# Gated cross-attention and a mixture of experts on one core: the first expert tile's copy, product and tanh set ahead of the fifteenth token tile's centring, and two experts' weights loaded in steps 10 to 12

## The chip, the core and the metric

The kernel runs on one core of one Trainium2 chip. The core has five engines that run their own instruction streams and meet at semaphores: TensorE (PE in the profile, with its weight loads as PEld), VectorE (DVE), ScalarE (ACT), GpSimd (POOL) and SyncE (SP). Transfers between the chip's memory and the core are issued from the streams of SP, ACT and POOL (SPq, ACTq and POOLq in the profile) and carried by 16 DMA engines. The metric is the device time of one execution in microseconds; lower is better.

## The reference, cut to what matters

There are 8 sequences of 256 tokens with 512 features: 2048 tokens. Each token attends to the memory rows that its sequence's mask leaves open, the result is added with a gate, and then each token passes through 2 of 8 experts.

```python
x = x + jnp.tanh(g_xattn[0]) * _L0_xattn_ref(_layernorm(x, axis=-1), ctx_2048, mask_BxS2_bk0)
x = x + jnp.tanh(g_ffn[0]) * _L0_ffn_ref(_layernorm(x, axis=-1), L0_ffn_w_router, L0_ffn_w_gate, L0_ffn_w_up, L0_ffn_w_down)

# _L0_ffn_ref, on xt of T = 2048 rows:
probs = jax.nn.softmax(xt @ w_router.T, axis=-1)
top_v, top_i = jax.lax.top_k(probs, TOP_K)                  # TOP_K = 2 of 8 experts
top_v = top_v / jnp.sum(top_v, axis=-1, keepdims=True)
comb = jnp.zeros((T, NUM_EXPERTS), dtype=xt.dtype)
comb = comb.at[jnp.arange(T)[:, None], top_i].add(top_v)
g = jnp.einsum('th,eih->tei', xt, w_gate)                   # 512 -> 192
u = jnp.einsum('th,eih->tei', xt, w_up)
act = jax.nn.silu(g) * u
out = jnp.einsum('tei,ehi,te->th', act, w_down, comb)       # 192 -> 512
```

## The kernel before

The work has two stages that overlap. In the token stage a loop over `s` from 0 to 17 takes the 16 tiles of 128 tokens through a software pipeline: tile `s + 1` gets its attention scores (`a_scores`), tile `s - 1` its probabilities (`a_probs`) and its values and sum (`a_values`), and tile `s - 2` is centred (`f_centre`) and squared for the variance (`f_square`). Once per two tiles `f_scale` and `f_weigh` complete the normalised rows, and `f_weigh` stores them with their routing weights into a table in the chip's memory, `xc_d`, by a DMA on ACT's queue (line 444). `f_mark`, `f_rank` and `f_table` build the lists that say which tokens belong to which expert.

In the expert stage each of 36 tiles holds up to 128 tokens of one expert. `gather` (line 639, POOL's queue) fetches a tile's rows from `xc_d` by an index list; `turn` transposes them on PE into `pt_g` (line 192) and copies the result to `xT_g` on ACT (line 194); `gate_up` multiplies with the gate and up weights on PE (line 659, `pgu`), takes a tanh on ACT (line 664) and two products on DVE (lines 665 and 667); `flip` transposes on PE (line 674, `pht`) and copies on DVE; `down` multiplies with the down weights (line 683, `py`), scales on ACT (line 688), and adds the rows into the output by an indirect DMA on POOL's queue (line 689). One call of `step(n)` issues `gate_up` of tile n, `flip` of tile n - 1, `turn` of tile n + 2 and `down` of tile n - 2.

The order of work on every engine is written out by hand: the code of `manual_schedule` is issued in program order, each engine takes its own instructions in that order, and an instruction that waits holds up all that stand behind it on its engine. Three places matter here.

- In step 16 (`s == NT`), `f_centre` and `f_square` of token tile 14 stand near the top, and `turn(order[0])`, the transposes and the copy of the first expert tile, after `a_values(15)`. In step 17, `gate_up(order[0])` and `turn(order[1])` come first, then `f_centre(15)` and `f_square(15)`. So on ACT the first tile's copy stands behind tile 14's centring and squaring.
- The tile lists for the first 8 expert tiles are made early, from the first 10 token tiles (`EARLY = 10`), whose rows are complete in `xc_d` after `f_weigh(4)` in step 13. The gathers of those tiles read only these rows and wait for that store. `fetch` in steps 13 to 16 issues them. The other tiles wait for `f_weigh(7)`, after the last token tile.
- The weights of an expert are loaded in two halves, `load_half(2e)` for gate and up (768 KB) and `load_half(2e + 1)` for down (384 KB). `LOADS` says in which step of the loop each of the first eight halves, those of experts 0 to 3, is issued on SP's queue: steps 3 to 8, and both halves of expert 3 in step 16. The other eight are issued on ACT's queue, one in each of the expert steps 0 to 7. On SP's queue the stores of the attention's result (`x_store`, line 623, two tiles each, in even steps) and the loads of the next sequence's `xT` (line 124) stand in the same program order; an `x_store` waits for DVE's sum of its second tile (line 414).

Of the kernel before, what the change touches and what calls it, by code (L numbers as in the profile page):

```python
# [22 lines left out]
E, I = 8, 192  # L23
T = B * S
TT = S // P
NT = T // P
# [22 lines left out]
def gated_xattn_moe(ctx: ExitStack, tc: tile.TileContext, x, xT, ctxn, ctxT, mask, maskT, g_x, g_f, wr, wgu, wd, out):  # L49
    nc = tc.nc  # L50
# [22 lines left out]
    def row(shape, name):  # L73
        return make(wk, 512, "row", 10, shape, name)
# [64 lines left out]

    def load_half(n):  # L140
        e, part = divmod(n, 2)
        by = nc.sync if n < E else nc.scalar
        if part == 0:
            by.dma_start(out=wgu_sb[:, e * GU:(e + 1) * GU], in_=wgu[:, e * GU:(e + 1) * GU])
        else:
            by.dma_start(out=wd_sb[:, e * DN:(e + 1) * DN], in_=wd[:, e * DN:(e + 1) * DN])
# [269 lines left out]
    def f_centre(i):  # L416
        xr = KEEP["xr", i // 2][:, i % 2, :]
        nc.scalar.activation(xr[:, 0:D], xs[i], AF.Identity, bias=xr[:, NM:NM + 1])  # L418

    def f_square(i):  # L420
        xr = KEEP["xr", i // 2][:, i % 2, :]
        if i % 2 == 0:
            KEEP["ve", i // 2] = sm_.tile([P, 2], FP, tag="ve", bufs=3, name=f"ve_{i}")
        square = row([P, D], f"sq_{i}")
        nc.scalar.activation(square, xr[:, 0:D], AF.Square, scale=2.0 / math.sqrt(D),
                             accum_out=KEEP["ve", i // 2][:, i % 2:i % 2 + 1])
# [198 lines left out]
    def on(f, i, n=NT):  # L625
        if 0 <= i < n:
            f(i)
# [15 lines left out]
    def turn(q):  # L643
        KEEP["xgT", q] = turned(KEEP["xg", q], f"g{q}")
# [4 lines left out]
    def gate_up(q):  # L649
        if q < NS:  # L650
            v = KEEP["own", q] = q if q < E else (q - E) // (LS - 1)
        else:
            v = nc.values_load(eqi[0:1, q - NS:q - NS + 1], engines=[PE], min_val=0, max_val=E - 1,
                               skip_runtime_bounds_check_because="a count of comparisons, at most E - 1")
        KEEP["v", q] = v
        xgT = KEEP.pop(("xgT", q))
        pgu = bank([P, 2 * I], f"pgu_{q}")
        for c in range(HC):
            nc.tensor.matmul(pgu, lhsT=xgT[:, c, :], rhs=span(wgu_sb, v * GU + c * 2 * I, 2 * I),  # L659
                             start=(c == 0), stop=(c == HC - 1))  # L660

        xg = KEEP["xg", q]
        th = half([P, I], f"th_{q}")
        nc.scalar.activation(th, pgu[:, 0:I], AF.Tanh, scale=xg[:, RS:RS + 1])  # L664
        nc.vector.scalar_tensor_tensor(th, th, 1.0, pgu[:, 0:I], ALU.add, ALU.mult)  # L665
        h = half([P, I], f"h_{q}")
        nc.vector.scalar_tensor_tensor(h, th, xg[:, R2:R2 + 1], pgu[:, I:2 * I], ALU.mult, ALU.mult)  # L667
        KEEP["h", q] = h
# [27 lines left out]
    order = [*range(E - 1)]  # L696
# [8 lines left out]
        if 0 <= s < len(order):  # L705
            f(order[s])

    LOADS = (3, 4, 5, 6, 7, 8, NT, NT)
    KEEP["next"], KEEP["known"] = 0, E - 2

    def fetch(upto):
# [3 lines left out]

    def step(s):
        fetch(s + AHEAD)
        if s < E:
            load_half(E + s)
        if s:  # L720
            at(gate_up, s)
        at(flip, s - 1)
        at(turn, s + 2)
        at(down, s - 2)
# [11 lines left out]
    with tc.manual_schedule(engines={PE, DVE, ACT, POOL, SP}):  # L736
        tc.mark_branch_hint_location("long", engines=[PE])
        m_find()
        m_hot(0)
        m_pick(0)  # L740
        m_rows(0, 1)
        m_fetch(0)
        m_count()
        nc.scalar.activation(tg, gates, AF.Tanh)
        constants()
        for p in range(1, NP):
            m_hot(p)
        a_stats(0)
        a_stats(1)
        a_scale(0)  # L750
        r_centre()
        m_hide(0)
        for p in range(1, NP):
            m_pick(p)
        m_rows(1, NP)
        idle = bank([P, D], "idle")
        for n in range(1):
            nc.tensor.matmul(idle, lhsT=ones, rhs=busy, start=True, stop=True)
        v = nc.values_load(many[0:1, 0:1], engines=[PE, DVE, ACT, POOL, SP], min_val=0, max_val=M,
                           skip_runtime_bounds_check_because="rows of a memory")  # L760
        with tc.If(v > CV, label="long") as cmp:
            apart.append({})
            long_way()
        apart.clear()
        with cmp.Else():
            nc.scalar.copy(xs[TT][:, 0:1], cns[0][:, 0:1])
            load_x(TT, 2 * TT)
            load_batch(2)
            load_x(2 * TT, NT // 2)
            load_x(NT // 2, NT)  # L770
        m_mean(0)
        m_centre(0)
        m_turn(0)
        m_gates()
        for s in range(NT + 2):
            odd = s % 2
            p, part = divmod(s, 4)
            on(a_probs, s - 1)
            if s == EARLY + 3:
                f_weigh(EARLY // 2 - 1)  # L780
            if s == EARLY + 2:
                f_close()
            if s == NT + 1:
                gate_up(order[0])
                turn(order[1])
            on(f_centre, s - 2)
            if s:
                if s == 1:
                    a_stats(4)
                on(a_stats, s + 4)  # L790
                if odd:
                    on(a_scale, (s + 3) // 2, NT // 2)
            on(a_scores, s + 1 if s else 0, NT)
            if s == 0:
                for n in range(1, NP):
                    m_fetch(n)
                m_hide(1)
                a_scores(1)
                a_stats(2)
                a_stats(3)  # L800
                a_scale(1)
                more_constants()
                m_route(0)
            if s in (1, 3, 5):
                m_hide(s + 1)
                m_hide(s + 2)
            if part == 1 and p + 1 < NP:
                m_centre(p + 1)
            on(f_square, s - 2)
            if odd:  # L810
                on(f_rank, (s - 3) // 2, NT // 2 - 1)
            if s == EARLY + 3:
                read_table(pick[:, 0:E], 0, E)
            if part == 2 and p + 1 < NP:
                m_turn(p + 1)
            on(a_values, s - 1)
            if s == NT:
                turn(order[0])
            if s == 1:
                nc.tensor.matmul(table, lhsT=ones[0:1, :], rhs=zero[:, 0:P], start=True, stop=True)  # L820
            if odd:
                on(f_weigh, (s - 5) // 2 if s != EARLY + 3 else -1, NT // 2 - 3)
            else:
                on(f_scale, (s - 4) // 2, NT // 2 - 1)
                on(f_mark, (s - 2) // 2, NT // 2 - 1)
                on(f_table, (s - 4) // 2, NT // 2 - 2)
            if s == NT - 4:
                last_constants()
            if s == NT - 2:
                place_rows()  # L830
            if s == EARLY + 1:
                f_total(EARLY // 2 - 1)
            if s == EARLY + 2:
                take_table("early")
            if s == 3:
                no_tokens()
            if s == NT + 1:
                step(0)
                f_weigh(NT // 2 - 3)
                f_weigh(NT // 2 - 2)  # L840
                f_table(NT // 2 - 2)
                f_rank(NT // 2 - 1)
                step(1)
                f_weigh(NT // 2 - 1)
                f_table(NT // 2 - 1)
                take_table("all")
                step(2)
                read_table(pick[:, E:NS], E, NS)
                KEEP["known"] = len(order) - 1
                step(3)  # L850
                f_total(NT // 2 - 1)
                step(4)
                numbers()
                step(5)
                read_table(sel, NS, NQ)
            if part == 0 and p + 1 < NP:
                m_mean(p + 1)
            if part == 0 and 0 < p < NP:
                m_route(p)
            if not odd:  # L860
                on(x_store, (s - 2) // 2, NT // 2)
            if not odd and 3 <= (s + 4) // 2 < B:
                load_batch((s + 4) // 2)
            for n in range(E):
                if LOADS[n] == s:
                    load_half(n)
            if NT - 3 <= s <= NT:
                fetch(2 * (s - NT + 3) + 1)
        for n in range(6, len(order) + 2):
            step(n)  # L870
        more_tiles()
# [31 lines left out]
```

## Time and profile before

| | us |
|---|---|
| three runs | 273.59, 275.84, 276.36 |
| median | 275.84 |
| the profiled execution, whole | 272.73 |
| its span from first to last instruction | 270.8 |
| PE busy | 241.9 (89%) |
| POOL busy | 151.0 (56%) |
| DVE busy | 111.3 (41%) |
| ACT busy | 109.3 (40%) |
| the first expert product (line 659) begins at | 79.76 |
| the last scatter (line 689) is issued at | 262.87 |
| data moved | 48.20 MB, 178 GB/s on average |

The profile is one execution. Its views are a page of sums; a timeline of each engine's instructions; a chain of waits, followed back from the last instruction to whatever released each step; tables of busy time in chosen windows, with the granted TensorE clock (1.00 is full speed) and the busy share of the DMA engines; and the instructions of one source line, with the time from a DMA's issue to its landing. A busy PE is not the same as a PE at its peak. Times inside the profile are counted from the span's start, and the profiled execution is 3.1 us below the median of the three timed ones.

### The profile page before, as it was taken

To read this page: it belongs to the slowest core of one execution; us is meant where nothing else is said; L and a number is where in the kernel's file an instruction comes from. 1 tells how busy PE (TensorE), PEld (TensorE's weight loads), DVE (VectorE), ACT (ScalarE), POOL (GpSimd) and SP (SyncE) were. 2 spreads that over 40 slices of the span, in tenths; PEclk is the share of its full clock that TensorE was granted. 3 is DMA by queue.
4 is the path that set the end of the run, shared out by engine and by line. 5 is a ranking of instruction groups with operands and counts; after the bars stand their busy time and mean duration, and the time that the engine had idled before them with its cause. 6 is when DMAs were issued, how large, how long until landed. Compare 5 with 4: busy or idle time off the path is not lost.

```text
span 270.8 us, 3452 instructions
## 1 busy us (share of the span) xinstructions
PE 241.9 (89%) x998; PEld 149.0 (55%) x998; DVE 111.3 (41%) x451; ACT 109.3 (40%) x264; POOL 151.0 (56%) x243
## 2 busy tenths in 40 slices
PE   4787788879759999999999999999999999999960
PEld 4585565657426655556556555565555555655520
DVE  3448888986974336412213213123122131131310
ACT  2224677777735533333323323333333233333230
POOL 4748899878684055334548384563745745333460
PEclk9999999999997999999999999999999999999995
DMA  4599779995389999884449395595674858326274
GB/s 118 198 340 365 252 236 342 333 336 232 101 273 317 385 312 304 221 178 95 83 82 159 92 168 95 106 173 101 111 155 82 138 112 143 61 39 81 40 94 68
DMA packets 18684, 48.20 MB, mean 178 GB/s; under 512 B 2528, under 2 KB 2528, under 8 KB 18656
## 3 DMA queue, kind: packets, MB, share of 16 engines
q0 software_dynamic: 8416, 21.11, 40.8%
q1 hardware_dynamic: 7040, 17.32, 18.6%
q10 hardware_dynamic: 3200, 9.44, 9.9%
q8 instruction: 12, 0.20, 0.3%
q14 instruction: 16, 0.13, 0.2%
HBM read 29.51 MB, written 18.35 MB: 177 GB/s over the span
## 4 chain that ended last, share of the span: by engine, by line
PE 68%; POOL 10%; DVE 7%; DMA 6%; issue 4%; ACT 3%; SPq 0%; POOLq 0%; ACTq 0%; DVEq 0%
PE pgu L659 34%; PE py L683 21%; PE pt_g L192 6%; POOL ac L491 5%; DMA xh<-x 4%; PE pht L674 3%; POOL out L689 2%; DMA cn<-ctxn,gid 2%; DVE xh L414 1%; PE psc L378 1%; POOL hide L301 1%; DVE st L362 1%; POOL rs L370 1%; PE pc L294 1%; DVE ac L491 1%
## 5 line engine op out<-in xcount | busy, mean ns | idle before, releaser
L659 PE MATMUL pgu<-wgu_sb,xT_g 128*128 128x384 f32 (+1 forms) x288 | 100.9, 494 | 2.9 <-ACT xT_g L194 2.9
L689 POOL DMA_INDIRECT out<-y,ids x36 | 57.1, 1585 | 80.4 <-ACT y L688 25.2
L659 PEld LDWEIGHTS pgu<-wgu_sb,xT_g 128*128 128x128 f32 x288 | 54.7, 192 | 46.7 <-issue 15.3
L683 PE MATMUL py<-wd_sb,hT 96*128 96x512 f32 (+1 forms) x144 | 67.6, 593 | 0.0
L665 DVE SCALAR_TENSOR_TENSOR th<-th,pgu 128x192 f32<-128x192 f32 x36 | 12.8, 354 | 122.7 <-ACT th L664 122.7
L664 ACT ACTIVATE th<-pgu,xh 128x192 f32<-128x192 f32 x36 | 15.1, 420 | 68.9 <-PE pgu L659 63.4
L639 POOL DMA_INDIRECT xh<-xc_d,gids x36 | 35.7, 993 | 12.4 <-issue 7.2
L688 ACT ACTIVATE y<-py,w 128x512 f32<-128x512 f32 x36 | 24.7, 687 | 39.9 <-PE py L683 39.0
L683 PEld LDWEIGHTS py<-wd_sb,hT 96*128 96x128 f32 x144 | 24.5, 190 | 17.8 <-issue 17.5
L194 ACT COPY xT_g<-pt_g 128x512 f32<-128x512 f32 x36 | 21.0, 584 | 8.9 <-PE pt_g L192 8.8
L378 PE MATMUL psc<-cT,xT 128*128 128x137 f32 x128 | 19.6, 302 | 2.5 <-POOL hide L301 1.1
L192 PE MATMUL pt_g<-ident,xh 128*128 128x128 f32 x144 | 21.6, 274 | 0.0
L378 PEld LDWEIGHTS psc<-cT,xT 128*128 128x128 f32 x128 | 17.9, 209 | 5.0 <-issue 2.2
L491 POOL TENSOR_SCALAR ac<-cols,low,idt 128x128 f16<-128x128 f32 x22 | 18.7, 862 | 1.7 <-DVE low L481 1.4
L192 PEld LDWEIGHTS pt_g<-ident,xh 128*128 128x128 f32 x144 | 17.1, 142 | 1.2 <-issue 1.0
L408 PE MATMUL pav<-cn,prT 128*128 128x512 f32 x32 | 16.4, 594 | 0.0
L674 PEld LDWEIGHTS pht<-ident,h 128*96 128x96 f32 x72 | 9.0, 126 | 12.3 <-issue 7.0
L667 DVE SCALAR_TENSOR_TENSOR h<-th,xh,pgu 128x192 f32<-128x192 f32 x36 | 14.9, 415 | 1.3
L509 POOL MEMSET spacer<- 1x1 f32 x25 | 15.2, 610 | 0.0
L676 DVE COPY hT<-pht 96x256 f32<-96x256 f32 x36 | 14.9, 413 | 0.4 <-PE pht L674 0.4
L418 ACT ACTIVATE xr<-xh,xr 128x512 f32<-128x512 f32 x16 | 11.6, 722 | 6.1 <-DVE xh L414 5.5
L674 PE MATMUL pht<-ident,h 128*96 128x128 f32 x72 | 13.8, 273 | 0.0
(187 smaller groups left out, 244.0 us busy)
## 6 DMA issues: line engine op xcount, KB each, us to landing
xc_d<-xr ACTq DMA_DIRECT2D x8, 576.0 KB, 5.2
xT<-xT SPq DMA_DIRECT2D x8, 512.0 KB, 5.9
out<-xh SPq DMA_DIRECT2D x8, 512.0 KB, 4.0
wgu_sb<-wgu SPq DMA_DIRECT2D x4, 768.0 KB, 7.5
wgu_sb<-wgu ACTq DMA_DIRECT2D x4, 768.0 KB, 6.0
xh<-x SPq DMA_DIRECT2D x1, 2048.0 KB, 14.2
wd_sb<-wd SPq DMA_DIRECT2D x4, 384.0 KB, 7.0
wd_sb<-wd ACTq DMA_DIRECT2D x4, 384.0 KB, 5.2
```

The costliest lines, as they stand in the source:

```text
L192: nc.tensor.transpose(pt[:, c, :], src[:, c * P:(c + 1) * P], ident)
L194: nc.scalar.copy(dst, pt)
L378: nc.tensor.matmul(both, lhsT=xTs[b][:, c, t * P:(t + 1) * P], rhs=cTs[p % 2][:, c, :], start=(c == 0), stop=(c == HC - 1))
L408: nc.tensor.matmul(pav, lhsT=prT, rhs=cns[p], start=True, stop=True)
L491: by.tensor_scalar(at_col[:, n, :], cols_w if by is nc.vector else cols, low[:, n:n + 1], idt[:, i, n % 2:n % 2 + 1], ALU.is_equal, ALU.mult)
L509: nc.gpsimd.memset(spacer, 0.0)
L639: nc.gpsimd.indirect_dma_start(out=g, out_offset=None, in_=src, in_offset=bass.IndirectOffsetOnAxis(ap=gids[:, q:q + 1], axis=0))
L659: nc.tensor.matmul(pgu, lhsT=xgT[:, c, :], rhs=span(wgu_sb, v * GU + c * 2 * I, 2 * I), start=(c == 0), stop=(c == HC - 1))
L674: nc.tensor.transpose(pht[:, k, :], h[:, k * IH:(k + 1) * IH], ident)
L683: nc.tensor.matmul(py, lhsT=hT[:, k, :], rhs=span(wd_sb, v * DN + k * D, D), start=(k == 0), stop=(k == 1))
L688: nc.scalar.activation(y, py, AF.Copy, scale=w)
L689: inst = nc.gpsimd.indirect_dma_start(out=out[:, :], out_offset=bass.IndirectOffsetOnAxis(ap=ids[:, q:q + 1], axis=0), in_=y, in_offset=No ...
```

## The change

Four edits, in two groups.

The order of ACT, PE and DVE in steps 16 and 17: `turn(order[0])` in step 16 is now followed at once by `gate_up(order[0])` and `turn(order[1])`, and only then by `f_centre(14)` and `f_square(14)`, which leave their old places in that step. Step 17 keeps `f_centre(15)` and `f_square(15)`. On ACT the order goes from centre 14, square 14, copy 0, tanh 0, copy 1, centre 15, square 15 to copy 0, tanh 0, copy 1, centre 14, square 14, centre 15, square 15. The orders of PE, DVE and POOL stay as they were.

The loads: ten halves instead of eight are issued on SP's queue in the loop. Those of expert 3 move from step 16 to steps 10 and 11, behind `x_store(4)` and the last `xT` load; those of expert 4 move from ACT's queue in expert steps 0 and 1 to SP's queue in step 12, between `x_store(5)` and `x_store(6)`. The remaining six halves stay on ACT's queue, in expert steps 0 to 5 instead of 2 to 7.

```diff
     def load_half(n):
         e, part = divmod(n, 2)
-        by = nc.sync if n < E else nc.scalar
+        by = nc.sync if n < len(LOADS) else nc.scalar
...
-    LOADS = (3, 4, 5, 6, 7, 8, NT, NT)
+    LOADS = (3, 4, 5, 6, 7, 8, 10, 11, 12, 12)
...
     def step(s):
         fetch(s + AHEAD)
-        if s < E:
-            load_half(E + s)
+        if len(LOADS) + s < 2 * E:
+            load_half(len(LOADS) + s)
...
-            if s == NT + 1:
-                gate_up(order[0])
-                turn(order[1])
-            on(f_centre, s - 2)
+            if s != NT:
+                on(f_centre, s - 2)
...
-            on(f_square, s - 2)
+            if s != NT:
+                on(f_square, s - 2)
...
             if s == NT:
                 turn(order[0])
+                gate_up(order[0])
+                turn(order[1])
+                f_centre(s - 2)
+                f_square(s - 2)
...
-            for n in range(E):
-                if LOADS[n] == s:
+            for n, when in enumerate(LOADS):
+                if when == s:
                     load_half(n)
```

## The prediction

> **What bounds the kernel now.** I read the page first, then the chain of waits around the first expert tile, then ACT's timeline there, then windows with clock and DMA share, and last the landing times of single DMAs. The page says that PE carries the end:
>
> ```profile
> PE 241.9 (89%) x998; PEld 149.0 (55%) x998; DVE 111.3 (41%) x451; ACT 109.3 (40%) x264; POOL 151.0 (56%) x243
> PE 68%; POOL 10%; DVE 7%; DMA 6%; issue 4%; ACT 3%; SPq 0%; POOLq 0%; ACTq 0%; DVEq 0%
> ```
>
> From 92 us on PE has no gap until 260 us, one tile every 4.96 us. Whatever brings PE to that stretch earlier or later moves the end by as much: the last scatters follow the last products, so the tail moves along. What matters is how PE gets into the stretch. The chain of waits from 77 to 92 us (start, length, what):
>
> ```profile
> 77.76 0.73 ACT xr L418
> ...
> 79.24 0.48 ACT xT_g L194
> 79.72 0.04 issue
> 79.76 4.43 PE pgu L659 x8
> ...
> 85.65 2.68 PE pgu L659 x8
> ...
> 91.86 0.42 PE pht L674 x2
> ```
>
> The first product waits for the copy of line 194, and the copy stands behind the centring of token tile 14 on ACT. The first product also takes 4.43 us where the second takes 2.68. ACT's timeline shows why the copy is late:
>
> ```profile
> 74.77 0.27 ACT L397 COPY prT<-ppt 128x128 f32<-128x128 f32 x1 [0.50 <-PE ppt L395]
> 77.76 0.72 ACT L418 ACTIVATE xr<-xh,xr 128x512 f32<-128x512 f32 x1 [2.73 <-DVE xh L414]
> 78.52 0.63 ACT L425 ACTIVATE sq<-xr 128x512 f32<-128x512 f32 x1
> ...
> 79.14 0.56 ACT L194 COPY xT_g<-pt_g 128x512 f32<-128x512 f32 x1
> 84.23 0.42 ACT L664 ACTIVATE th<-pgu,xh 128x192 f32<-128x192 f32 x1 [4.53 <-PE pgu L659]
> ```
>
> ACT idles 2.73 us for DVE's sum of tile 14, though the transposes for the copy are done at 76.87 in PE's timeline. The slow product is a matter of the clock (windows; the columns are PE, PEld, DVE, ACT, POOL busy, granted clock, DMA share, GB/s):
>
> ```profile
> 77.46:80.87 3.41, 1.11 (x4) 0.71 (x5) 2.33 (x11) 1.91 (x4) 2.76 (x4) 1.00 0.76 219
> 80.87:84.28 3.41, 3.41 (x8) 1.76 (x7) 0.00 (x0) 0.05 (x1) 2.01 (x4) 0.50 0.94 292
> ```
>
> After a window of 3.41 us in which PE was busy 1.11, the clock is halved for the next 3.41.
>
> **Part 1, the order on ACT.** Nothing is added; the same instructions run in another order. If the rows come as before, the copy starts at 76.9 instead of 79.14, takes 0.56, and the product starts near 77.5: -2.25 us. The two passes that stood ahead (centre and square of tile 14, 77.76 to 79.14, 1.38 us) now stand behind tanh 0 and copy 1. Queued behind them are centre and square of tile 15, copy 2, the three `f_weigh`, and tanh 1. Before, square 15 ends at 86.74, which lets DVE make the last lists until 88.50 and PE take them at 88.82, a slack of 0.3; tanh 1 at 90.55 lets PE flip at 91.86 with no slack (the weight load there waits 0.63 us for DVE's `h`). All of these come 1.38 later after the end of product 0: +1.38 us, with no cover. Centring 14 itself is needed by no one earlier.
>
> **Part 2, the loads in steps 10 to 12.** SP issues 768 and 384 KB behind the `xT` load at 58.65, so at about 59.1 to 60, and as much again behind the store of 64.87, at about 65.3 to 66.5. Together 2.36 MB. At the 396 GB/s of the full window 51 to 53.5 us that is 6.0 us of all DMA engines. They have this much room before:
>
> ```profile
> 62.00:64.00 2.00, 1.76 (x10) 0.92 (x9) 1.79 (x11) 1.45 (x5) 2.00 (x4) 1.00 0.69 269
> 64.00:66.00 2.00, 1.58 (x15) 1.53 (x14) 1.01 (x5) 1.20 (x4) 1.84 (x6) 1.00 0.25 95
> 66.00:68.00 2.00, 1.98 (x15) 1.50 (x15) 1.07 (x8) 1.80 (x8) 1.07 (x8) 1.00 0.57 222
> ```
>
> Idle share times 2 us: 0.62 + 1.50 + 0.86, with 0.1 before and 0.4 after, 3.5 us. So 2.5 us of load work is still outstanding when ACT issues the store of `f_weigh(4)` at 67.86. On this store hangs the first gather, which is now critical: the store lands 2.9 us after issue, at 70.76; the gather starts at 71.66, and its rows land 4.1 later, at 75.76; PE's first weight load for the transposes is at 75.84. Before, these rows waited 2.3 us for ACT; that cover is what Part 1 removes. How does a store fare that is issued behind loads? The same store two steps earlier tells (line 444, issued at 47.0 behind loads of 44.1 to 45.8, and at 67.9 behind none):
>
> ```profile
> L444 ACTq DMA_DIRECT2D xc_d<-xr x1: 379/379/379, 47.0 to 47.0; - x1
> ...
> DMA to landing us min/median/max: 7.8/7.8/7.8
> ```
>
> ```profile
> L444 ACTq DMA_DIRECT2D xc_d<-xr x1: 369/369/369, 67.9 to 67.9; - x1
> ...
> DMA to landing us min/median/max: 2.9/2.9/2.9
> ```
>
> And in the DMA view of 46 to 50 us only SP's queue moves packets:
>
> ```profile
> q1 hardware_dynamic: 308, 1.12, 101.0%
> ```
>
> ACT's store (q10) got nothing until SP's loads were through. **A rule speaks otherwise:** the Trainium skill, "DMA: Bandwidth & Descriptors", section "Queues, rings and completion order", says that each DMA engine goes round-robin between the queues that have work. Then the store, 0.59 MB or 1.5 us, would share half and half and come 1.5 us late. By the trace, first issued first moved, it comes 2.5 late. I take 2.5, the trace's case; the bounds are 0 and 3.0 (none of the last idle usable). With 2.5: gather at 74.16, rows at 78.26, first load 78.34, transposes done about 79.1 (0.60 for four, and 0.14 for the first load), copy 0.56, product at 79.7. Against 79.76: -0.05 us. By the rule it would be 78.7, -1.05. So Parts 1 and 2 together leave PE waiting for rows where it waited for ACT. POOL is also held: `f_scale(5)` and the later gathers start 2.5 later; the third (75.79) then lands at about 82.2, and PE asks for it at about 82.4 at the earliest.
>
> What the loads relieve: SP's loads at 80.55 and 81.06 and two on ACT go from the stretch where the DMA share is 1.0. PE waits for no DMA there before, so this gives nothing by itself. ACT's issue of a `wd` half at 89.60 took 0.84 us, the other three on ACT 0.33 to 0.35, and it stands ahead of tanh 1; with fewer transfers it may shrink: between 0 and -0.5, I take -0.25. Expert 3's and 4's weights are needed from 94.6 and 99.7 us; earlier arrival gains nothing.
>
> **The clock.** Until 76.43 PE is busy, then come 0.6 us of transposes and nothing until 79.7: in 77.46 to 80.87 there would be 0.6 of transposes and 1.2 of product. The windows before show 1.00 kept after 1.99 busy in 3.41 and 0.50 after 1.11; 1.8 lies between. The skill's "TensorE: Matmul & The Clock Gate", Part 4 ("PE-mode transpose"), says that transposes do not count as busy in the same way: then 1.2, and the clock drops as before. I take no change, 0; bounds -1.75 (4.43 against 2.68) and +1.7 (a second window).
>
> **Sum:** -0.05 + 1.38 - 0.25 + 0 = +1.1 us. The profiled execution would go from 272.73 (span 270.8 and 1.9 around it) to 273.8. It lies 3.1 under the median of the runs, 275.84; moved by the same, the median becomes 276.9.
>
> **The rivals.**
> - *Faster: the rows are not late.* The store overtakes or shares, and the product starts between 77.5 and 78.7. Then the window is filled with 2.2 us or more of product, the clock holds, and the sum is -2.25 + 1.38 - 0.25 - 1.75 = -2.9 (273.0), or by sharing -1.05 + 1.38 - 0.25 - 1.75 = -1.7 (274.2). For it: the rule above. Against: the 7.8 us landing. 0.27.
> - *Slower: the first gather also meets the store of tiles 12 and 13.* That store is issued at 72.67 and held the second gather (73.11) to 5.4 us where others take 3.9 to 4.1. The first gather at 74.16 may take its place: +1.3, and with the larger backlog +0.5. Product at 81.5, PE without products for 5 us, which can hold a whole window and so a second one at half clock, +1.7: 1.1 + 1.8 + 1.7 = +4.6, 280.4. It decides once the rows land after 79. Against it: by 74.16 plus the gather's own start most of that store is through. 0.20.
> - *The forecast, but with the clock held:* +1.1 - 1.75, 275.2. It is part of the forecast's 0.53.
>
> That the change doesn't do what it says is excluded: in the instruction lists of both kernels only ACT's four passes and the loads have moved.
>
> **How the numbers follow.** About 1% is what a measurement of this kernel can tell from no change: 273.1 and 278.6. Faster by more: half of the first rival and a little spread, 0.2. Slower by more: the second rival and the upper end of the forecast, 0.3. Within: 0.5. The range runs from the first rival's better end, 273.0, to most of the second, 279.8.
>
> **What would show it.** Right: the first gather starts near 74 and not at 71.7; the store of line 444 issued near 67.9 lands 5 us after issue or later; PE waits ahead of the first transposes, not after them; product 0 begins at 79 to 80; tanh 1 begins 7.5 us or more after product 0 ends, not 6.35. Wrong: product 0 begins before 78.5, or takes 2.7 us, or the store lands in 3 to 4 us. If the step from product 0 to the flip of tile 1 does not grow by 1.1 or more, the cost of the reordered passes is wrong.

## The result: slower, and PE waits for rows that stand behind the loads

| | before | after |
|---|---|---|
| median of 15 executions, us | 275.43 | 278.30 |
| lowest to highest, us | 271.87 to 277.54 | 276.88 to 281.05 |
| ratio of the times | | 1.0151, 95% interval 1.0112 to 1.0189 |
| the profiled execution, whole, us | 272.73 | 277.40 |
| its span, us | 270.8 | 275.6 |

The ratio leaves out executions over 1.5% above the fastest of their kernel, four of before's fifteen and one of after's, so it says +4.1 us where the medians of all fifteen stand 2.9 apart.

The page of the changed kernel (engine, busy us, share, count; then the chain's shares by engine; then two groups with busy us, mean ns and the idle time ahead of them):

```profile
PE 243.1 (88%) x998; PEld 149.5 (54%) x998; DVE 111.2 (40%) x451; ACT 109.3 (40%) x264; POOL 150.7 (55%) x243
...
PE 63%; POOL 10%; DMA 7%; issue 6%; ACT 5%; DVE 4%; ACTq 1%; SPq 1%; POOLq 0%; DVEq 0%
...
L659 PE MATMUL pgu<-wgu_sb,xT_g 128*128 128x384 f32 (+1 forms) x288 | 100.9, 494 | 0.7 <-ACT xT_g L194 0.7
...
L192 PE MATMUL pt_g<-ident,xh 128*128 128x128 f32 x144 | 21.5, 273 | 3.3 <-DMA xh<-xc_d,gids 3.3
```

PE does the same work in almost the same busy time. The new thing is in the last line: all 3.3 us that PE idles ahead of the expert transposes end with a gather's landing. The chain of waits of the changed kernel (start, length, what) shows where that sits, and what follows it:

```profile
68.74 1.40 DMA xc_d<-xr
...
76.96 3.54 DMA xh<-xc_d,gids
80.50 0.14 issue
80.64 0.64 PE pt_g L192 x4
81.28 0.02 issue
81.30 0.59 ACT xT_g L194
81.89 0.04 issue
81.94 4.42 PE pgu L659 x8
...
86.38 0.42 ACT th L664
...
87.30 0.73 ACT xr L418
88.03 0.02 issue
88.06 0.72 ACT sq L425 x2
...
93.02 0.97 ACTq L146
...
94.09 0.43 ACT th L664
```

Three things are to be seen. Before, the last link ahead of the copy of line 194 was ACT's centring of tile 14; now it is the gather, then transposes and copy with no more than 0.14 us between them. Ahead of the gather POOL stands still for 6.04 us, waiting for the store that was issued at 68.74 (the chain shows only its first 1.40 us and then follows POOL). And after tanh 0 the two passes of tile 14 (87.30 to 88.7) now lie on the chain ahead of tanh 1. How long that store took to land is told by the instructions of line 444:

```profile
L444 ACTq DMA_DIRECT2D xc_d<-xr x1: 370/370/370, 68.7 to 68.7; - x1
...
DMA to landing us min/median/max: 7.3/7.3/7.3
```

It was 2.9 us before and is 7.3 now. POOL issues the first gather 0.9 us after this landing in both kernels, so it starts 8.22 us after the store's issue where it started 3.80 after it.

**Where the time went.** Executions reach the store of line 444 at different times (67.86 to 71.73 us in the profiles of this case, whichever the kernel), so stages are compared from that store's issue on. Before to after: tanh 0 from 16.37 to 17.64 us (+1.27), tanh 1 from 22.69 to 25.35 (+2.66), product 3 from 26.56 to 29.22 (+2.66). From there on PE runs both kernels at the same pace: the last scatter is issued at 262.87 and 266.41, 3.54 apart, which is these 2.66 and the 0.88 by which the store itself was issued later (67.86 and 68.74). So the two profiles put 2.66 us ahead of product 3.

Another 1.2 us of the 4.8 between the spans lie behind the issue of the last scatter: the last two scatters landed 7.2 and 6.7 us after their issue, where those of before took 5.8 and 5.4. In the other nine profiles of this case 7.8 to 8.1 us lie between the last scatter's issue and the end, in this one 9.2. Since neither part of the change alone has such a tail (8.1 with the loads alone, 7.8 and 8.1 with the order alone), it is not shown that the change makes it. What the ratio's 4.1 us have above 2.66 stays open. And a profile is one execution: in a second profile of the kernel before, shown further down, product 3 came 1.2 us later than in the first.

### The profile page after: what moved, and what is told of

Its sections match the earlier page's. It is cut to its first block, busy times and chain, and to the rows that moved or that the text cites. A ratio compares the mean times of both kernels' runs of the same rounds, so it can differ in the third digit from the quotient of the medians.

```text
span 275.6 us, 3453 instructions
## 1 busy us (share of the span) xinstructions
PE 243.1 (88%) x998; PEld 149.5 (54%) x998; DVE 111.2 (40%) x451; ACT 109.3 (40%) x264; POOL 150.7 (55%) x243
## 4 chain that ended last, share of the span: by engine, by line
PE 63%; POOL 10%; DMA 7%; issue 6%; ACT 5%; DVE 4%; ACTq 1%; SPq 1%; POOLq 0%; DVEq 0%
PE pgu L659 32%; PE py L683 21%; PE pt_g L192 5%; POOL ac L491 5%; DMA xh<-x 4%; PE pht L674 3%; DMA cn<-ctxn,gid 2%; POOL out L689 2%; DMA xh<-xc_d,gids 1%; DVE st L362 1%; POOL hide L301 1%; POOL rs L370 1%; ACT xr L418 1%; PE pc L294 1%; ACT sq L425 1%
```

## The experiments

Five kernels tell the parts apart; two of them and the kernel before itself were run a second time ("again"). "From the store" means from the issue of the store of line 444 in the same execution.

| kernel | store lands after | first gather starts, from the store | product 0 starts, from the store | product 0 takes | tanh 0 to tanh 1 | product 3, from the store | ratio to before (95%) |
|---|---|---|---|---|---|---|---|
| before | 2.9 | 3.80 | 11.90 | 4.43 | 6.32 | 26.56 | |
| after | 7.3 | 8.22 | 13.20 | 4.41 | 7.71 | 29.22 | 1.0151 (1.0112 to 1.0189) |
| order alone | 2.9 | 3.79 | 9.69 | 2.85 | 7.21 | 23.66 | 0.9934 (0.9894 to 0.9973) |
| loads alone | 7.5 | 8.41 | 13.79 | 5.09 | 6.45 | 29.24 | 1.0087 (1.0046 to 1.0128) |
| order, expert 3 early | not in the trace | 4.64 | 11.58 | 4.54 | 7.54 | 27.57 | 0.9996 (0.9960 to 1.0031) |
| order, expert 4 early | 6.0 | 6.92 | 11.89 | 4.54 | 7.25 | 27.59 | 1.0036 (0.9988 to 1.0084) |
| passes ahead of tanh 0 | not in the trace | 3.79 | 9.69 | 2.85 | 6.07 | 22.52 | 1.0006 (0.9950 to 1.0061) |
| before, again | 2.9 | 3.80 | 11.91 | 5.49 | 6.49 | 27.79 | 0.9966 (0.9925 to 1.0007) |
| order alone, again | 2.9 | 3.79 | 9.69 | 2.85 | 7.22 | 23.66 | 0.9932 (0.9892 to 0.9972) |
| passes ahead of tanh 0, again | not in the trace | 3.79 | 11.33 | 2.85 | 6.04 | 24.12 | 0.9951 (0.9913 to 0.9989) |

**The order alone.** The theory: without the loads the store is on time, and the new order brings what it can. The rival: the order costs by itself.

```diff
-    LOADS = (3, 4, 5, 6, 7, 8, 10, 11, 12, 12)
+    LOADS = (3, 4, 5, 6, 7, 8, NT, NT)
```

> Only the new order on ACT; the loads stand as in the kernel before. Queue theory (the loss is the store of f_weigh(4) standing behind the early loads, and the order alone is good): the first gather starts 3.8 us after the store is issued, as before; product 0 begins 9.7 us after that store's issue instead of 11.9 and takes 2.7 us instead of 4.4, since PE's gap is too short to halve the clock; tanh 1 begins 7.7 us after product 0 ends instead of 6.35. Sum -2.2 - 1.7 + 1.4 = -2.5 us, ratio 0.991. Rival (the reordered ACT passes are the whole loss): slower than the kernel before, by 1.4 us or more, ratio 1.005 to 1.015.

PE's timeline in this kernel (start, length, instruction, idle time ahead and what ended it):

```profile
77.71 1.02 PE L408 MATMUL pav<-cn,prT 128*128 128x512 f32 x2
78.57 0.60 PE L192 MATMUL pt_g<-ident,xh 128*128 128x128 f32 x4
79.84 2.85 PE L659 MATMUL pgu<-wgu_sb,xT_g 128*128 128x384 f32 x8 [0.67 <-issue]
```

The transposes follow PE's own token work without a gap, the product starts 0.67 later, and it takes 2.85 us, at full clock: in this trace the granted clock is 1.00 from 31.4 us until after 260. ACT's timeline shows the price as well:

```profile
82.73 0.42 ACT L664 ACTIVATE th<-pgu,xh 128x192 f32<-128x192 f32 x1 [2.94 <-issue]
...
83.65 0.72 ACT L418 ACTIVATE xr<-xh,xr 128x512 f32<-128x512 f32 x1
84.40 0.63 ACT L425 ACTIVATE sq<-xr 128x512 f32<-128x512 f32 x1
...
89.36 0.48 ACTq L146 DMA_DIRECT2D wd_sb<-wd  x1
89.94 0.42 ACT L664 ACTIVATE th<-pgu,xh 128x192 f32<-128x192 f32 x1 [1.02 <-issue]
```

Start -2.21, clock -1.58, tanh 1 +0.89: -2.9 us by product 3. The forecast held: product 0 began 9.69 us after the store's issue and took 2.85, tanh 1 began 7.25 after product 0 ended (7.7 had been expected), and the ratio was 0.9934. The order alone is a gain, and the rival fell. The median was 272.47 against 275.05.

**The loads alone.** The order of before, the ten `LOADS` of after (the edits of steps 16 and 17 undone).

```diff
             if s == NT:
                 turn(order[0])
-                gate_up(order[0])
-                turn(order[1])
-                f_centre(s - 2)
-                f_square(s - 2)
```

> Only the early loads; the order on ACT as in the kernel before. Queue theory: the store lands 7.3 us after issue and the first gather starts about 8.2 after it, as with the whole change; product 0 begins 13.2 after the store's issue instead of 11.9, at half clock again; the passes of tile 14 are done in the wait, so tanh 1 stays at 6.35 after product 0. Sum +1.3 us, ratio 1.005. Rival 1 (only the order costs): ratio 1.000. Rival 2 (the early transfers cost by themselves, elsewhere): the whole loss, ratio 1.013 or more.

The store lands 7.5 us after its issue, as in after, and product 3 comes as late (29.24 against 29.22). The way there is another than in after: here the product took 5.09 us, over two half-clock windows, while tanh 1 is not held up (6.45 us behind tanh 0, where after has 7.71). The kernel before also had two such windows in one of its profiles and one in the other, so the equal 29.2 is in part chance: with one window the loads alone would have come some 0.7 us sooner (5.09 - 4.41, an estimate).

Taken together: by product 3 the order gives -2.9, the loads +2.68, and both +2.66. The gain of the order is not there to be set against the loss: with rows that late it doesn't matter what stands ahead of the copy on ACT, and only the order's price, the passes ahead of tanh 1, is left. The times lean the same way, 1.0087 without the new order and 1.0151 with it, though the two intervals overlap. The ratio lies between the forecast's 1.005 and the second rival's 1.013 and does not part them; by the trace the loss comes ahead of product 3 and begins with the store's late landing. The first rival fell.

**One expert's loads at a time.** If the bytes ahead of the store are what delays it, the pair just ahead of it (expert 4, step 12) should cost most of the delay, and the pair of steps 10 and 11 (expert 3) little.

```diff
-    LOADS = (3, 4, 5, 6, 7, 8, 10, 11, 12, 12)
+    LOADS = (3, 4, 5, 6, 7, 8, 10, 11)
```

> The new order, and only expert 3's two halves early, in steps 10 and 11; expert 4's stay on ACT's queue. Queue theory: 1.18 MB are through before the store of f_weigh(4) is issued, so that store lands 3 to 4 us after its issue, product 0 begins 9.7 to 10.7 after it, ratio 0.990 to 0.995. Rival (any early load delays the store, half of the bytes half of the delay): the store lands 5 us after issue, product 0 begins 11.5 after it, ratio 1.002 or more.

The forecast of this run failed in the product's time and the ratio. The gather started 4.64 us after the store's issue, only 0.84 later than in before, so the rival's late landing (5 us) did not come either. But PE's timeline shows this:

```profile
79.96 0.63 PE L192 MATMUL pt_g<-ident,xh 128*128 128x128 f32 x4 [1.70 <-DMA xh<-xc_d,gids]
81.26 4.54 PE L659 MATMUL pgu<-wgu_sb,xT_g 128*128 128x384 f32 x8 [0.68 <-ACT xT_g L194]
```

The rows of a gather started at 74.32 were used at 79.96, 5.6 us later; in after and in the next kernel it is 3.7. The store of the attention's result of tiles 12 and 13 (line 623) was issued at 74.50, 0.2 us behind this gather. In before it was the second gather that started 0.44 us from that store, and it took 5.4 us. So 0.84 us of delay became 1.9 us at the product (11.58 against 9.69), and the product ran at half clock again (4.54 us). That the meeting with this store is the cause is read from the traces; no run moved the store away.

```diff
-    LOADS = (3, 4, 5, 6, 7, 8, 10, 11, 12, 12)
+    LOADS = (3, 4, 5, 6, 7, 8, NT, NT, 12, 12)
```

> The new order, and only expert 4's two halves early, in step 12 (behind the output store of tiles 10 and 11, just ahead of the store of f_weigh(4)); expert 3's stay in step 16. First issued, first moved: the store of f_weigh(4) waits for all that is left of these 1.18 MB and lands 5 to 6 us after its issue; product 0 begins 11.5 to 12.5 after that issue, at half clock, tanh 1 7.5 after product 0 ends: ratio 1.003 to 1.008. Rival (turn by turn between the queues): the store lands 4 us after issue at most, product 0 begins by 10.8 after it, ratio 0.995 or less.

The instructions of line 444 in this kernel:

```profile
L444 ACTq DMA_DIRECT2D xc_d<-xr x1: 369/369/369, 68.1 to 68.1; - x1
...
DMA to landing us min/median/max: 6.0/6.0/6.0
```

The forecast held: landing 6.0, product 0 at 11.89 and at half clock, tanh 1 7.29 us after its end, ratio 1.0036. With 1.18 MB issued just ahead of it the store lands after 6.0 us, with 2.36 MB after 7.3, with none after 2.9. Half of the bytes make 3.1 of the 4.4 us of delay: the later pair weighs more, as the theory has it. Either half alone puts product 3 3.9 us later than the order alone has it and brings the ratio back to about 1.00, so it eats all that the order gives. Against before (26.56 and 27.79) product 3 is then no clear loss.

**The passes between the copy and tanh 0.** The order alone still pays for two passes ahead of tanh 1. While product 0 runs, ACT is idle; this kernel sets them there (the old `LOADS`).

```diff
             if s == NT:
                 turn(order[0])
-                gate_up(order[0])
-                turn(order[1])
                 f_centre(s - 2)
                 f_square(s - 2)
+                gate_up(order[0])
+                turn(order[1])
```

> Loads as before; on ACT copy 0, then centre and square of tile 14, then tanh 0 and copy 1. The two passes lie in the time in which ACT waits for product 0. Queue theory with the passes as a cost of their own: product 0 as in the run with the order alone (9.7 us after the store's issue, 2.7 long), tanh 1 at 6.35 after its end: -4.0 us, ratio 0.986, 1.4 us better than the order alone. Rival (the passes behind tanh 0 cost nothing, since PE finds other work): the same as the order alone.

ACT's timeline:

```profile
80.78 0.58 ACT L194 COPY xT_g<-pt_g 128x512 f32<-128x512 f32 x1 [1.88 <-PE pav L408]
81.64 0.72 ACT L418 ACTIVATE xr<-xh,xr 128x512 f32<-128x512 f32 x1 [0.27 <-issue]
82.39 0.63 ACT L425 ACTIVATE sq<-xr 128x512 f32<-128x512 f32 x1
...
84.31 0.42 ACT L664 ACTIVATE th<-pgu,xh 128x192 f32<-128x192 f32 x1 [1.19 <-PE pgu L659]
```

The passes lie beside the product and still leave 1.19 us of idle time ahead of tanh 0. Tanh 0 to tanh 1 goes from 7.21 to 6.07 us and product 3 from 23.66 to 22.52: they cost 1.14 where they stood, in the trace. The times don't show it, and the forecast of 0.986 failed: 1.0006, with single executions from 272.35 to 280.83 us, where the order alone had 271.06 to 275.02.

**Three kernels again.** The kernel before, this last one and the order alone, beside each other.

> The kernel before, unchanged, timed as a version of its own: ratio 1.000, with the interval that a comparison of this kernel with itself has. If the spread of its runs (272 to 279 us) lies in the token stage, as theory says, the issue of the f_weigh(4) store stands at another time than 67.86 in this profile, by 0.5 us or more, and product 0 again begins 11.9 us after it.

> The passes of tile 14 between copy 0 and tanh 0 once more. In its first profile tile 3's product came 22.5 us after the f_weigh(4) store's issue, 4.2 sooner than before and 1.1 sooner than with the order alone, but the store was issued at 71.7 and the runs spread from 272 to 281. Theory (the token stage's spread, which this edit doesn't touch, hid the gain): the ratio comes out between 0.984 and 0.993 this time. Rival (the edit itself makes executions slower somewhere else): 1.000 again, with the same wide spread.

> The order alone once more, beside the version with the passes between: ratio 0.993 as before, within 0.004; if the token stage's spread moves whole comparisons, it differs by more than that.

The kernel before against itself gave 0.9966 (0.9925 to 1.0007): a comparison here moves by 0.3% with nothing changed. Its forecast held: the store was issued at 69.03 instead of 67.86, and product 0 began 11.91 us after it. The order alone repeated its ratio, 0.9932 (0.9892 to 0.9972), and every step of its profile to within 0.05 us.

The passes beside the product gave 0.9951 (0.9913 to 0.9989), again spread from 271.21 to 280.81: short of the forecast (0.984 to 0.993), better than the rival's 1.000. So it is not shown that this kernel is faster than the order alone. In both of its sets of runs the executions above 279 us are the ones with the lowest mean granted clock (0.964 to 0.966, against 0.970 to 0.990 in the others). Its second profile has a half-clock window ahead of the product, which then started 11.33 us from the store, though the first profile and both of the order alone had 9.69 (windows; busy us of PE, PEld, DVE, ACT, POOL, granted clock, DMA share, GB/s):

```profile
72.71:76.12 3.41, 1.82 (x10) 0.95 (x9) 3.03 (x17) 2.71 (x10) 3.00 (x5) 1.00 0.46 97
76.12:79.53 3.41, 3.31 (x8) 1.77 (x8) 3.17 (x15) 0.06 (x1) 2.64 (x4) 0.50 0.84 287
```

The window ahead of the half-clock one had PE busy for 1.82 us. Why this kernel meets such windows more often than the order alone, if it does, is open.

How uneven the clock is even with the kernel unchanged is seen in the second profile of the kernel before:

```profile
76.73:80.14 3.41, 1.31 (x7) 0.54 (x5) 3.10 (x17) 1.17 (x2) 2.64 (x4) 1.00 0.85 288
80.14:83.55 3.41, 2.61 (x4) 1.50 (x5) 1.06 (x4) 0.75 (x3) 2.81 (x6) 0.50 0.88 259
83.55:86.96 3.41, 3.41 (x9) 1.96 (x8) 0.04 (x1) 0.42 (x1) 0.78 (x1) 0.50 1.00 309
```

Two half-clock windows, not one, and the first product took 5.49 us instead of 4.43. That is 1.06 of the 1.23 us by which its product 3 came later than in the first profile. What one profile says of product 3 can be off by that much: against this second profile the change's +2.66 would be +1.43 and the order's -2.9 would be -4.1. The signs stand in both, and the ratios bear them out. Some of the spread of before's times may come from here; the profile of one execution can't say how often it happens.

The version that beats both is the order alone: 0.7% below before in both of its comparisons, and, by the two ratios (0.9934 / 1.0151), 2.1% below after.

## Why the forecast held, and where it was off

**The new wait: right.** The forecast said that PE would wait ahead of the first transposes, for rows behind a late store, and no longer behind them for ACT. That is what the chain shows, and the part kernels show that it is the loads which bring it: 7.5 us of landing with the loads alone, 2.9 with the order alone. Two of the signs named ahead missed, both on account of the next term: the gather started at 76.96 and not near 74, product 0 at 81.94 and not at 79 to 80. The others came.

**The size of the store's delay: the mis-sized term.** It was taken as 2.5 us, with 3.0 as the upper bound; measured 4.4 (7.3 - 2.9). The gather so started 8.22 us after the store where the forecast had 6.30; the rows then came 3.5 after it instead of 4.1; and the product started +1.3 us against before (from the store) where the sum said -0.05. The working let all idle room of the DMA engines, 3.5 us, be used at 396 GB/s, so that 1.4 of the 2.36 MB were through at the store's issue and 1.0 MB, 2.5 us, outstanding. The windows of the nine us ahead of the store's issue (before, then after; columns as above) say otherwise:

```profile
58.86:67.86 9.00, 8.33 (x57) 6.18 (x57) 6.09 (x37) 6.23 (x24) 7.10 (x19) 1.00 0.66 248
59.74:68.74 9.00, 8.33 (x57) 6.19 (x57) 6.39 (x37) 6.52 (x24) 7.30 (x20) 1.00 0.96 318
```

The engines were busy for 2.7 us more (0.30 of nine), and they moved only 0.63 MB more (70 GB/s for nine us): the room was smaller than reckoned, and the rate lower. Two windows of after show the rate at its lowest:

```profile
62.00:64.00 2.00, 1.76 (x12) 1.50 (x13) 1.79 (x10) 1.36 (x6) 2.00 (x3) 1.00 1.10 335
64.00:66.00 2.00, 1.58 (x11) 0.96 (x10) 1.82 (x11) 1.60 (x6) 1.92 (x4) 1.00 0.85 260
```

Here a full share moved 305 GB/s (335 / 1.10, 260 / 0.85), where the same two windows of before moved 380 to 390 per full share (269 / 0.69, 95 / 0.25), and the window of 70 to 72 us in after 413 (430 / 1.04). The 396 had been read off a window of stores and loads two stages earlier. Why the loads moved more slowly in 62 to 66 is open.

The rest shows in the queues' view of after, from the store's issue on (packets, MB, share of the 16 engines' time; q1 is SP's queue, q10 ACT's), for 68.74 to 70, 70 to 72, 72 to 74 and 74 to 76 us:

```profile
q1 hardware_dynamic: 191, 0.40, 80.4%
q10 hardware_dynamic: 66, 0.12, 25.0%
...
q1 hardware_dynamic: 206, 0.86, 104.4%
...
q1 hardware_dynamic: 111, 0.40, 56.3%
q10 hardware_dynamic: 144, 0.33, 45.0%
...
q1 hardware_dynamic: 247, 0.49, 64.1%
q10 hardware_dynamic: 128, 0.26, 33.0%
```

The 0.12 MB are the end of the store before this one. With them, 1.78 MB that had been issued earlier moved from the store's issue to 74 us, instead of the 1.0 MB of the forecast; at 396 GB/s they are 4.5 us, and the delay was 4.4. So the wait was right and the work ahead of the store was taken too small.

**First issued, first moved: it described the wait, and the rest is open.** The Trainium skill, "DMA: Bandwidth & Descriptors", section "Queues, rings and completion order", has each DMA engine take turns between the queues that it has work for; the prediction made of this a store that shares half and half from its issue on and lands 1.5 us late, an estimate. That did not come: from 70 to 72 us SP's queue moved alone, and the store's first data packet moved at 72.25, 3.5 us after its issue (0.9 in before). The landings of 6.0 and 7.3 us behind 1.18 and 2.36 MB say the same, and so the first rival, rows not late, fell. From 72.25 on both queues moved packets, and the store took 3.3 us from its first packet to its last where it took 1.7 in before, alone. The view adds up 16 engines, so it doesn't tell whether each of them took turns then, as the page has it, or whether some were through with the loads before others. For the store of 47 us in the kernel before the prediction reads that it got nothing until SP's loads were through. That holds to 51 us; from 51 to 52 both queues move there, with one of these loads landing only at 53.2:

```profile
q1 hardware_dynamic: 56, 0.28, 68.7%
q10 hardware_dynamic: 43, 0.10, 25.0%
```

**The passes: right.** Predicted +1.38 from tanh 0 to tanh 1, less 0.25 for a shorter issue of `wd`; measured +1.39 (6.32 to 7.71). The issue did not shrink (0.97 against 0.84 us), so the passes themselves cost 1.26; moving them away from there saved 1.14 in the kernel with the passes ahead of tanh 0. The 0.25 for the issue is the other term that was wrong, and small. The same issue took 0.58 us in the second profile of before and 0.48 with the order alone, so its length was not known to 0.25 us.

**The clock: right, and in part by luck.** No change was taken; product 0 took 4.41 against 4.43 us. The windows of the changed kernel:

```profile
78.30:81.71 3.41, 0.63 (x4) 0.42 (x4) 2.43 (x11) 0.41 (x1) 3.02 (x5) 1.00 0.63 173
81.71:85.12 3.41, 3.18 (x5) 1.85 (x6) 0.00 (x0) 0.17 (x1) 2.50 (x4) 0.50 0.85 267
```

A window with 0.63 us of transposes and nothing else is followed by one at half clock, as one with 1.11 was before. Since 0.63 is low in any case, this does not test whether transposes count. And the number of half-clock windows was not the forecast's to know: with the same late rows the loads alone had two of them (product 0 took 5.09 us), and before had two in its second profile.

**The slower rival** needed the first gather to meet the output store of tiles 12 and 13. In after the gather started 3.4 us behind that store (73.55) and landed in 3.5, so it did not happen there: a longer delay carried the gather past the collision. It did happen in the kernel with expert 3 early.

**Sum.** +1.27 and +1.39 by the profiles, 2.66 us, where the forecast had +1.1; the missing 1.6 us are +1.32 for the rows (in tanh 0) and +0.26 for the `wd` issue and the passes. The medians stand 2.9 us apart and the ratio says 4.1, so the middle of the forecast was too small by more than half. That 278.30 still lies in the range of 273.0 to 279.8 is owed to the width of that range, which had been left open for other outcomes; the mechanism is what the forecast had right.

## What to carry to other kernels

Moving work out of the way of a wait pays only as far as the next thing in line allows, and that next thing has to be followed to its source: here rows, a gather, a store, and what was issued to the DMA engines in the 8 us before that store. A load that nobody waits for is not free when a store that somebody waits for is issued behind it; here half of the bytes already cost 3.1 us of landing and cancelled the gain. So test the two parts of such a change apart: together they hid a version that is faster than either.

## What the runs showed of the hardware

- A store of 0.59 MB on ACT's queue, issued behind loads on SP's queue, waited for most of them: it landed after 2.9 us with nothing ahead, 6.0 behind 1.18 MB, 7.3 and 7.5 behind 2.36 MB. Its first data packet moved 0.9, 3.0 and 3.5 us after the issue; from then on packets of both queues moved in the same time.
- At a DMA share near 1.0 the engines moved between 305 GB/s (62 to 66 us) and 413 GB/s (70 to 72 us) per full share in one profile: a full share is not one rate.
- A gather that starts earlier need not bring its rows earlier by as much: the one started 4.64 us after the store, 0.2 us ahead of another store, brought its rows to PE in 5.6 us, the ones started 6.92 and 8.22 after it in 3.7. That the other store is the cause is not shown by a run.
- In the ten profiles, between 20 and 260 us, every window of 3.41 us at full clock with PE busy 1.46 us or less was followed by one at half clock, every one with 1.99 or more by one at full clock; between 1.58 and 1.98 both occurred. Of the twelve half-clock windows the ten with PE busy 3.06 us or more were followed by full clock, the two with 2.2 and 2.6 by another at half clock.
